# The opening of a two-layer transformer kernel: normalisation in parts, another order of loads and stacks

## The chip, the cores and the metric

The kernel runs on one NeuronCore of a Trainium2 chip. Its time is device microseconds of one execution, and the median of three runs stands for the kernel. In what follows PE is TensorE (PEld its weight load), DVE VectorE, ACT ScalarE, POOL GpSimd and SP SyncE; SPq and ACTq are the queues in which SP and ACT issue DMAs.

## The reference

Two layers act on x of 2048 tokens by 128 channels. Each has an attention and a feed-forward part, each behind a normalisation that is modulated by six vectors from a conditioning vector c:

```python
mod = (silu(c) @ wmod).reshape(1, 6, 1, 128)            # sa, ca, ga, sb, cb, gb
ga = (2 * (ga >= 0) - 1) * maximum(abs(ga), 0.25)       # gb likewise
h = layernorm(x) * (1 + ca) + sa
x = x + ga * attention(h)
h = layernorm(x) * (1 + cb) + sb
x = x + gb * feed_forward(h)
```

Layer 0's attention has 16 heads of 8 channels, is not causal and has biases; its feed-forward part routes each token to one of 16 experts and adds a shared expert. Layer 1's attention is causal, with 8 query heads that share one key and one value head; its feed-forward part mixes each token with the one before. Everything is float32.

## The kernel before, in words

**Opening (L48 to L165).** x goes into SBUF in four blocks of 512 tokens, on SP and ACT in turn (L50 to L52). `load` (L54) brings the small vectors `vec`, the modulation weights `wmod0` and `wmod1` (L65) and 17 weights; 17 of these 20 DMAs are issued on POOL (L59 to L83), and after them POOL makes the identity (`ident`, L89) and the other constants. `last_rows` (L101) is a column with a one in each row 31, 63, 95 and 127. Then (L140 to L164) both layers' modulations are computed: a sigmoid on ACT, six matmuls for each layer (L149, one column each; a float32 matmul stands as two instructions in the records), a copy, two additions and five small steps for each of the two gates on DVE.

**First normalisation.** `layernorm_T` (L168) takes statistics of all 16 tiles of 128 tokens on DVE (L177, L178), one square root on ACT (L179), a reciprocal, and then for each block of four tiles the normalised values (L186), four transposes on PE (L188) and one ACTIVATE with scale and shift into `hT` (L189).

**Layer 0's attention.** `begin0` (L604) makes what the attention reads. Keys are split into a high part and the rest (`split`, L237: hi on ACT, L243; lo on DVE, L244), so that a matmul of rounded operands keeps float32's accuracy. `kS` holds eight *stacks* of 128 rows by 2048 tokens, each for two heads. A stack is first filled with `last_rows` over all its columns (L608, DVE and POOL in turn), and then `stack` (L254) writes four sets of 16 rows into it by DMA (L258): hi, lo, hi, lo of two heads' keys, 128 KB each, 32 in all. hi and lo lie in the memory of `stacks[1]`, which later holds queries. Values are projected by 32 instructions on PE (L631) and a bias added on DVE (L634). `project_q` (L342) does the same as for keys for a block of 512 queries: project (L346), split, and 32 DMAs of 32 KB into `qS`, after a memset on POOL for the first two blocks (L353). hi and lo of a block of queries lie in one buffer each (`qh`, `ql`), so the next block's split waits until these DMAs have read them.

`attention` (L284) works in 16 units, each a block of 512 queries and a group of four heads. Group g reads stacks 2g and 2g+1. The first pass of a unit has 32 steps: two score matmuls on PE (L375, four instructions' worth of 512 columns at most in three PSUM buffers) and a maximum on DVE (L379). Its maxima are then turned (L408) and copied (L409), and SP writes them into the query stack (L412). The second pass computes scores again (L440), takes the exponential on ACT (L450) and weighs the values on PE (L466). `look_ahead` (L557) interleaves them: while unit u makes its second pass, unit u+1 makes its first, and eight steps more (`LEAD`) before unit u's second pass begins. So the first unit's first pass has nothing beside it. A list `late` gives small pieces of other work to every second step; its first entry, in the first unit, is `fold0` (L672), which multiplies the output weights by the gate: two matmuls into a free bank (`fold_gate`, L267, L273), a product on DVE (L275), a copy on ACT (L277), and four additions to x on POOL (L282). `project_q` of the next block is called in the second group's first pass.

**What sets the order.** [...]The framework that builds the program fills these queues by a plan of its own, not in the order of the code: in the trace the product at L271 for layer 1's gate, which the code asks for at the end of layer 0, runs on DVE at 17.07 us between two statistics of the first normalisation.

Of the kernel before, what the change touches and what calls it, by code (L numbers as in the profile page):

```python
# [18 lines left out]
P = 128  # L19
T = 2048  # L20
# [22 lines left out]
def two_layers(ctx: ExitStack, tc: tile.TileContext, a: dict, out: bass.AP):  # L43
# [4 lines left out]
    x = const.tile([P, NT, P], F32, name="x")  # L48
    xv = a["x"].rearrange("(t p) c -> p t c", p=P)
    for b in range(NB):  # L50
        eng = nc.sync if b % 2 == 0 else nc.scalar
        eng.dma_start(out=x[:, b * TB:(b + 1) * TB, :], in_=xv[:, b * TB:(b + 1) * TB, :])  # L52
# [6 lines left out]
    vec = load("vec", [P, NV], nc.gpsimd)  # L59
    modw = ctx.enter_context(ExitStack())  # L60
    wmodp = modw.enter_context(tc.tile_pool(name="wmodp", bufs=1))
    wmod = []
    for layer in range(2):
        t = wmodp.tile([P, 6 * P], F32, name=f"wmod{layer}_sb", tag=f"wmod{layer}")
        nc.gpsimd.dma_start(out=t, in_=a[f"wmod{layer}"])  # L65
        wmod.append(t)
    wk0 = load("wk0", [P, P], nc.sync)
    wv0 = load("wv0", [P, H0 * VW], nc.scalar)
    bv0 = load("bv0", [P, H0 * VW], nc.gpsimd, a["bv0"].partition_broadcast(P))
    wq0 = load("wq0", [P, P], nc.sync)  # L70
    wo0 = load("wo0", [P, P], nc.gpsimd)
    wr0 = load("wr0", [P, NE], nc.gpsimd)
    wsg = load("wsg", [P, NS * P], nc.gpsimd)
    wsu = load("wsu", [P, NS * P], nc.gpsimd)
    wsd = load("wsd", [P, NS, P], nc.gpsimd)
    wk1 = load("wk1", [P, P], nc.gpsimd)
    wv1 = load("wv1", [P, W], nc.gpsimd)
    wq1 = load("wq1", [P, P], nc.gpsimd)
    wq1s = load("wq1s", [P, 4, P], nc.gpsimd)
    wo1 = load("wo1", [P, P], nc.gpsimd)  # L80
    wfr = load("wfr", [P, P], nc.gpsimd)
    wfk = load("wfk", [P, P], nc.gpsimd)
    wfv = load("wfv", [P, P], nc.gpsimd)  # L83
# [5 lines left out]
    ident = const.tile([P, P], F32, name="ident")  # L89
    make_identity(nc, ident)  # L90
    eps = const.tile([P, 1], F32, name="eps")
    nc.gpsimd.memset(eps, 1e-5)
# [6 lines left out]

    last_rows = const.tile([P, 1], F32, name="last_rows")  # L100
    nc.vector.tensor_reduce(last_rows, ident[:, 31::32], AX.X, ALU.add)  # L101
# [35 lines left out]

    mods = []  # L140
    with tc.tile_pool(name="modp", bufs=2, space=PSUM) as mp:
        sg = const.tile([P, 2], F32, name="sg")
        nc.scalar.activation(sg, vcol(V_C0, 2), AF.Sigmoid)
        sc = const.tile([P, 2], F32, name="sc")
        nc.vector.tensor_mul(sc, sg, vcol(V_C0, 2))
        for layer in range(2):
            ps = mp.tile([P, 6], F32, name=f"mod_ps{layer}", tag="mod_ps")
            for j in range(6):
                nc.tensor.matmul(ps[:, j:j + 1], wmod[layer][:, j * P:(j + 1) * P],  # L149
                                 sc[:, layer:layer + 1], start=True, stop=True)  # L150
            m = const.tile([P, 6], F32, name=f"mod{layer}", tag=f"mod{layer}")
            nc.vector.tensor_copy(m, ps)
            for j in (1, 4):
                nc.vector.tensor_scalar_add(m[:, j:j + 1], m[:, j:j + 1], 1.0)
            for j in (2, 5):
                g = m[:, j:j + 1]
                sign = const.tile([P, 1], F32, name=f"sign{layer}{j}", tag=f"sign{layer}{j}")
                nc.vector.tensor_scalar(sign, g, 0.0, 2.0, ALU.is_ge, ALU.mult)
                nc.vector.tensor_scalar_add(sign, sign, -1.0)
# [917 lines left out]
```

## Time and profile before

| | us |
|---|---|
| median of three runs | 1306.71 |
| lowest and highest | 1306.31, 1310.28 |
| the profiled execution | 1276.53 |
| its span, first to last instruction | 1274.8 |

The span is what the profile's views divide; the profiled execution's own time is 1.7 us more. Times in a trace are counted from the start of the span. A group of instructions is given with its number, its busy time and the mean duration of one, where queueing behind others can be part of a duration. The chain of waits follows the work that ended last back from the end; what stands in it set the time.

| from the trace | start us | length us |
|---|---|---|
| first statistics (L177) | 4.39 | 0.26 each |
| identity begun on POOL | 13.46 | 0.22 and 0.32 |
| last block of hT (L189) | 25.91 | 0.78 |
| fills of kS on DVE | 25.91 | 9.71 |
| fills of kS on POOL | 25.95 | 11.43 |
| first key DMA on SP, on ACT | 31.69, 38.08 | |
| first score matmul (L375) | 60.24 | |
| turn of the first unit's maxima (L408) | 101.74 | 1.11 |
| first score of the second pass (L440) | 106.10 | |

### The profile page before, as it was taken

The page shows a single profiled execution, that of the slowest core. Times are in us where ns is not written, and L with a number is a line of the kernel's source. Part 1 is how long each engine was busy: PE and PEld are TensorE (multiplying, and loading weights), DVE is VectorE, ACT ScalarE, POOL GpSimd, SP SyncE. Part 2 cuts the span into 40 slices and gives each one's busy share as a digit, 9 for nine tenths or more (in the row PEclk, how much of TensorE's full clock was granted, in tenths as well). Part 3 has the DMA queues.
Part 4 walks back from the last instruction along what each step waited for, and adds up shares of the span by engine and source line. Part 5 has one row for each costly group of instructions (what it writes and reads, how often), then busy time and mean ns, then how long its engine had stood idle before and what let it go on. Part 6 is the DMA issues. An engine that isn't in the chain of part 4 may idle for free.

```text
span 1274.8 us, 22344 instructions
## 1 busy us (share of the span) xinstructions
PE 1154.6 (91%) x9243; PEld 522.7 (41%) x9243; DVE 967.3 (76%) x1495; ACT 762.8 (60%) x846; POOL 133.6 (10%) x194
## 2 busy tenths in 40 slices
PE   5279999999999999999999999977877999999985
PEld 3223334344333444443344333445643444444432
DVE  5499988899889889888889883173468878898224
ACT  2005777777777777777777778732313455656763
POOL 6401000000000000000000000026251111100113
PEclk9657999999999999999999999987987899999998
DMA  3810000001000001000000000042411001000001
GB/s 115 152 30 18 2 2 2 2 2 35 2 2 1 2 6 32 1 2 2 1 2 2 1 2 2 1 132 54 69 40 34 22 13 35 1 1 1 2 1 33
DMA packets 23700, 27.37 MB, mean 21 GB/s; under 512 B 4960, under 2 KB 17536, under 8 KB 23088
## 3 DMA queue, kind: packets, MB, share of 16 engines
q1 hardware_dynamic: 18512, 16.20, 5.1%
q0 software_dynamic: 2336, 5.48, 2.2%
q10 hardware_dynamic: 2752, 4.27, 1.6%
q8 instruction: 73, 1.20, 0.4%
q14 instruction: 27, 0.22, 0.1%
HBM read 9.88 MB, written 4.13 MB: 11 GB/s over the span
## 4 chain that ended last, share of the span: by engine, by line
PE 76%; DVE 11%; POOL 4%; DMA 3%; issue 3%; ACT 2%; SPq 0%; POOLq 0%; DVEq 0%; ACTq 0%
PE a0bank L466 23%; PE a0p L440 17%; PE a0p L375 12%; PE a1bank L466 5%; PE a1p L440 4%; DVE a0mx L379 3%; PE a1p L375 2%; DVE a1mx L379 2%; PE a1p L446 2%; POOL xs L859 2%; DVE a1masked L384 2%; DMA kS<-a0qS 1%; ACT a0e L450 1%; PE sg L773 1%; POOL kS L608 1%
## 5 line engine op out<-in xcount | busy, mean ns | idle before, releaser
L379 DVE TENSOR_REDUCE a0mx<-a0p 128x2 f32<-128x1024 f32 x512 | 623.7, 1225 | 84.9 <-PE a0p L375 75.6
L450 ACT ACTIVATE a0e<-a0p 128x1024 f32<-128x1024 f32 x512 | 522.3, 1025 | 173.1 <-PE a0p L440 147.2
L466 PE MATMUL a0bank<-a0e,vA 128*32 128x256 f32 x4096 | 333.3, 391 | 0.6 <-ACT a0e L450 0.6
L375 PE MATMUL a0p<-kS,a0qS 64*128 64x512 f32 x1024 | 248.4, 481 | 34.9 <-DMA a0qS<-a0ql 16.8
L440 PE MATMUL a0p<-a0qS,kS 64*128 64x512 f32 x1024 | 259.8, 497 | 0.2 <-DVE a0mx L379 0.2
L450 ACT ACTIVATE a1e<-a1p 128x1024 f32<-128x1024 f32 (+3 forms) x160 | 143.2, 897 | 93.2 <-PE a1p L446 90.3
L440 PEld LDWEIGHTS a0p<-a0qS,kS 64*128 64x128 f32 x1024 | 97.1, 184 | 204.9 <-issue 127.5
L375 PEld LDWEIGHTS a0p<-kS,a0qS 64*128 64x128 f32 x1024 | 100.3, 192 | 120.6 <-ACT a0e L450 58.0
L466 PEld LDWEIGHTS a0bank<-a0e,vA 128*32 128x32 f32 x4096 | 86.3, 108 | 138.6 <-issue 123.8
L379 DVE TENSOR_REDUCE a1mx<-a1p 128x2 f32<-128x1024 f32 x96 | 115.5, 1223 | 18.5 <-PE a1p L375 17.7
L466 PE MATMUL a1bank<-a1e,vA 128*32 128x256 f32 (+1 forms) x1152 | 96.2, 382 | 0.5 <-POOL a1e L453 0.4
L440 PE MATMUL a1p<-a1qS,kS 64*128 64x512 f32 (+3 forms) x320 | 75.1, 463 | 3.6 <-DVE a1mx L379 1.9
L924 POOL MEMSET vA<- 128x16 f32 x1 | 0.1, 127 | 717.9 <-PE a0bank L518 717.9
L375 PE MATMUL a1p<-kS,a1qS 64*128 64x512 f32 (+3 forms) x320 | 67.2, 421 | 6.9 <-DVE a1mx L384 3.9
L384 DVE CUSTOM_DVE_ANT_0 a1masked<-a1p,later 128x128 f32<-128x128 f32 (+3 forms) x128 | 62.6, 489 | 11.9 <-PE a1p L375 7.0
L446 PE MATMUL a1p<-a1mT,a1ones 64*128 64x512 f32 (+3 forms) x320 | 60.6, 371 | 0.0
L440 PEld LDWEIGHTS a1p<-a1qS,kS 64*128 64x128 f32 x320 | 30.7, 187 | 60.6 <-issue 33.4
L453 POOL TENSOR_SCALAR_AFFINE_SELECT a1e<-a1e 128x256 f32<-128x256 f32 x64 | 26.0, 406 | 229.9 <-ACT a1e L450 229.9
L375 PEld LDWEIGHTS a1p<-kS,a1qS 64*128 64x128 f32 x320 | 31.7, 193 | 35.0 <-DVE a1mx L384 9.1
L466 PEld LDWEIGHTS a1bank<-a1e,vA 128*32 128x32 f32 x1152 | 25.2, 108 | 42.1 <-issue 31.7
L446 PEld LDWEIGHTS a1p<-a1mT,a1ones 64*128 64x128 f32 x320 | 31.3, 191 | 1.3 <-issue 1.0
L859 POOL DMA_INDIRECT xs<-hs_rows,tok x31 | 29.6, 955 | 20.3 <-DVE tok L840 11.2
(328 smaller groups left out, 766.1 us busy)
## 6 DMA issues: line engine op xcount, KB each, us to landing
kS<-a0qS SPq DMA_DIRECT2D x16, 128.0 KB
kS<-a0qS ACTq DMA_DIRECT2D x16, 128.0 KB
wgu_sb<-in_gate_up SPq DMA_DIRECT2D x1, 2048.0 KB
a0qS<-a0qh SPq DMA_DIRECT2D x56, 32.0 KB
a0qS<-a0ql SPq DMA_DIRECT2D x56, 32.0 KB
y_rows<-y SPq DMA_DIRECT2D x7, 256.0 KB
a1qS<-a1qh SPq DMA_DIRECT2D x24, 64.0 KB
a1qS<-a1ql SPq DMA_DIRECT2D x24, 64.0 KB
```

Of the source, the lines that this page charges most:

```text
L375: nc.tensor.matmul(ps[:, j, :n], qS[b][r:r + RT, st, i * P:(i + 1) * P], kS(st)[r:r + RT, kb * QB:kb * QB + n], start=True, stop=True)
L379: nc.vector.tensor_reduce(pm[:, i, 2 * pair:2 * pair + 2, kb], ps, AX.X, ALU.max)
L384: nc.vector.tensor_tensor_reduce(masked[:, :n], ps[:, j, :n], later[:, QB - n:], 1.0, LOWEST, ALU.add, ALU.max, pm[:, i, g, kb:kb + 1])
L440: nc.tensor.matmul(ps[:, j, q0:], kS(st)[r:r + RT, kt * P:(kt + 1) * P], qS[b][r:r + RT, st, q0:], start=True, stop=fused)
L446: nc.tensor.matmul(ps[:, j, q0:], ones[r:r + RT, g // S, :], shift[u][r:r + RT, q0:], start=False, stop=True)
L450: nc.scalar.activation(e[:, :, q0:], ps[:, :, q0:], AF.Exp, scale=scale)
L453: nc.gpsimd.affine_select(out=e[:, :, q0:q0 + P], in_=e[:, :, q0:q0 + P], compare_op=ALU.is_ge, fill=0.0, base=0, pattern=[[0, 2], [1, P]] ...
L466: nc.tensor.matmul(av[g * W:(g + 1) * W, c0:c1], vA(kt, grp * HG + g), held[kt, g // 2][:, g % 2, c0:c1], start=(kt == 0 and c0 == 0), sto ...
L608: (nc.vector if st % 2 else nc.gpsimd).tensor_copy(kS[:, st, :], last_rows.to_broadcast([P, T]))
L773: nc.tensor.matmul(ps[:, j, :], w[:, k * P:(k + 1) * P], hT[:, b * QB:(b + 1) * QB], start=True, stop=True)
L859: nc.gpsimd.indirect_dma_start(out=xs[:, j, :], out_offset=None, in_=a["hs_rows"], in_offset=bass.IndirectOffsetOnAxis(ap=tok[:, j:j + 1], ...
L924: nc.gpsimd.memset(vA1[:, :, D1:D1 + 1], 1.0)
```

## The change

- Loads: none on POOL. SP and ACT issue them in order of need: x's first block, `vec`, the second block, `wmod0`, the third and fourth, then the key and query weights on ACT and all others on SP. `wmod0` and `wmod1` are kept for the whole kernel. `ident`, `eps` and `last_rows` come first on their engines.
- Fills: `kS0` is allocated ahead of the normalisation. All eight fills are ACTIVATEs on ACT (`fill`), two of them before the normalisation, six between the stacks.
- First normalisation: `first_norm` replaces `layernorm_T` here. For each of the four blocks `start` takes statistics and a square root, `end` the reciprocal, values, transposes and the ACTIVATE; block b+1 is started ahead of b's end. PSUM holds two blocks.
- Modulation: layer 0's (`modulation(0)`) stands after the first `start`; its gates come at the end of `begin0`. Layer 1's, with its gates, is computed in `fold0`, in the bank that `fold_gate` uses.
- Stacks: the first block's queries are projected and stacked in `begin0`, next to the keys. Stacks 0 and 1 use SP and ACT, the other six SP alone, in order of stack: four key DMAs, then four query DMAs. The memset for the first block's query stack stands at the beginning of `begin0`.

The core of the diff:

```diff
-    for b in range(NB):
-        eng = nc.sync if b % 2 == 0 else nc.scalar
-        eng.dma_start(out=x[:, b * TB:(b + 1) * TB, :], in_=xv[:, b * TB:(b + 1) * TB, :])
...
-        nc.gpsimd.dma_start(out=t, in_=a[f"wmod{layer}"])
...
+    load_x(0, nc.sync)
+    vec = load("vec", [P, NV], nc.scalar)
+    load_x(1, nc.scalar)
+    wmod = [load("wmod0", [P, 6 * P], nc.sync)]
+    load_x(2, nc.sync)
+    load_x(3, nc.scalar)
+    wk0 = load("wk0", [P, P], nc.scalar)
+    wq0 = load("wq0", [P, P], nc.scalar)
+    wv0 = load("wv0", [P, H0 * VW], nc.sync)
+    bv0 = load("bv0", [P, H0 * VW], nc.sync, a["bv0"].partition_broadcast(P))
+    wmod.append(load("wmod1", [P, 6 * P], nc.sync))
...
+    def modulation(layer, ps):
+        if layer == 0:
+            nc.scalar.activation(sg, vcol(V_C0, 2), AF.Sigmoid)
+            nc.vector.tensor_mul(sc, sg, vcol(V_C0, 2))
+        for j in range(6):
+            nc.tensor.matmul(ps[:, j:j + 1], wmod[layer][:, j * P:(j + 1) * P],
+                             sc[:, layer:layer + 1], start=True, stop=True)
+        m = const.tile([P, 6], F32, name=f"mod{layer}", tag=f"mod{layer}")
+        nc.vector.tensor_copy(m, ps[:, :6])
+        for j in (1, 4):
+            nc.vector.tensor_scalar_add(m[:, j:j + 1], m[:, j:j + 1], 1.0)
+        mods.append(m)
...
-            kS, vA, q0 = begin(ep, ps_s, stacks)
+            qS = {}
+            kS, vA, qS[0] = begin(ep, ps_s, stacks)
...
-                          (nc.sync, nc.scalar) if b == 0 else (nc.sync,), step)
+                          (nc.sync,), step)
...
-    layernorm_T(h, HOFF, m[:, 1:2], m[:, 0:1], "ln0")
...
+    def first_norm():
+
+        with tc.tile_pool(name="ln0", bufs=2) as wp, \
+                tc.tile_pool(name="ln0p", bufs=2, space=PSUM) as pp:
+            got = {}
+
+            def start(b):
...
+                for i in range(TB):
+                    nc.vector.bn_stats(stats[:, i, :], x[:, b * TB + i, :])
+                    nc.vector.bn_aggr(mv[:, i, :], stats[:, i, :])
+                rstd = wp.tile([P, TB], F32, name=f"ln0rstd{b}", tag="rstd")
+                nc.scalar.activation(rstd, mv[:, :, 1], AF.Sqrt, bias=eps)
+                got[b] = mv, rstd
+
+            def end(b):
+                mv, rstd = got.pop(b)
+                nc.vector.reciprocal(rstd, rstd)
+                xn = normal(b, f"ln0{b}", mv, rstd)
+                turn_normal(pp.tile([P, QB], F32, name=f"ln0ps{b}", tag="ps"), xn,
+                            hT[:, b * QB:(b + 1) * QB], mods[0][:, 1:2], mods[0][:, 0:1])
+
+            start(0)
+            modulation(0, pp.tile([P, 6], F32, name="mod_ps", tag="mod_ps"))
+            for b in range(NB):
+                if b + 1 < NB:
+                    start(b + 1)
+                end(b)
...
+    kS0 = pool.tile([P, H0 * RT // P, T], F32R, name="kS0", tag="kS")
+
+    def fill(st):
+
+        nc.scalar.activation(kS0[:, st, :], last_rows.to_broadcast([P, T]), AF.Copy)
+
+    for st in range(2):
+        fill(st)
+    first_norm()
...
-        for st in range(nst):
-            (nc.vector if st % 2 else nc.gpsimd).tensor_copy(kS[:, st, :],
-                                                             last_rows.to_broadcast([P, T]))
+        kS = kS0
+        nc.gpsimd.memset(stacks[0].bitcast(F32), 0.0)
...
+        ps = pp.tile([P, 2, QB], F32, name="pq0", tag="s")
+        nc.tensor.matmul(ps[:, 0, :], wq0, hT[:, :QB], start=True, stop=True)
+        split(ps[:, 0, :], vcol(V_BQ), qhi, qlo)
...
-            stack(kS[:, st, :], (hi[rows], lo[rows]), (0, 1, 0, 1), (nc.sync, nc.scalar), RT // D0)
+            queues = (nc.sync, nc.scalar) if st < 2 else (nc.sync,)
+            if st >= 2:
+                fill(st)
+            stack(kS[:, st, :], (hi[rows], lo[rows]), (0, 1, 0, 1), queues, RT // D0)
+            stack(stacks[0][:, st, :], (qhi[rows], qlo[rows]), (0, 0, 1, 1), queues, RT // D0)
...
+        gates(0)
...
     def fold0(bank):
+        modulation(1, bank)
+        gates(1)
         wog, rows = fold_gate(pool, bank, wo0, vcol(V_BO), m[:, 2:3], "a0")
```

## The prediction

> **What bounds the kernel now.** I read the page first, then busy time by stretches of time, then the chain of waits from 24 to 62 us, then the queues of SP and ACT. The page: TensorE is the bound of the whole.
>
> ```profile
> span 1274.8 us, 22344 instructions
> PE 1154.6 (91%) x9243; PEld 522.7 (41%) x9243; DVE 967.3 (76%) x1495; ACT 762.8 (60%) x846; POOL 133.6 (10%) x194
> PEclk9657999999999999999999999987987899999998
> ```
>
> An average hides stages. Stretches of layer 0 (columns: stretch, length, busy us with number of instructions for PE, PEld, DVE, ACT, POOL, granted clock, DMA share, GB/s):
>
> ```profile
> 26.00:38.00 12.00, 6.06 (x18) 3.04 (x16) 12.00 (x7) 3.50 (x4) 12.00 (x6) 0.90 0.41 63
> 38.00:56.00 18.00, 5.44 (x25) 5.17 (x24) 4.12 (x11) 0.00 (x0) 4.10 (x3) 0.59 0.96 182
> 61.00:103.00 42.00, 30.09 (x81) 11.34 (x80) 41.93 (x40) 0.80 (x2) 0.91 (x1) 0.50 0.13 29
> 120.00:290.00 170.00, 168.72 (x1494) 67.84 (x1492) 151.91 (x141) 128.29 (x130) 0.00 (x0) 1.00 0.01 2
> ```
>
> From 120 us on PE is busy 168.7 of 170 us: a unit of attention takes about 44.8 us there, and nothing of this change takes TensorE work out of it. Before that, in turn: DVE and POOL full (26 to 38), DMA full with PE nearly empty (38 to 56), DVE full at half clock (61 to 103, the first unit's first pass, whose maxima nobody has computed ahead). So the opening 60 us is a chain of its own, and what it loses shifts everything behind it. The chain of waits there:
>
> ```profile
> 25.95 11.43 POOL kS L608 x4
> 38.08 4.38 DMA kS<-a0qS
> 42.53 4.44 DMA kS<-a0qS
> 47.05 5.14 DMA kS<-a0qS
> 52.27 3.20 DMA kS<-a0qS
> 58.35 1.90 DMA a0qS<-a0ql
> 60.25 0.80 PE a0p L375 x2
> ```
>
> POOL fills kS for 11.4 us, then 32 key transfers of 128 KB come in rounds of eight, about 4.4 us each, then the query stacks. The first unit reads only two of the eight stacks. The fills (mean of one in ns) and the modulation:
>
> ```profile
> L608 POOL CAST kS<-last_rows 128x2048 fp32r<-128x2048 f32 x4 | 11.4, 2892 | 3.6 <-PE ln0ps L188 3.6
> L608 DVE CAST kS<-last_rows 128x2048 fp32r<-128x2048 f32 x4 | 9.7, 2488 | 1.9 <-PE ln0ps L188 1.9
> L149 PE MATMUL mod_ps<-sc,wmod_sb 128*128 128x1 f32 x24 | 5.3, 352 | 8.3 <-DMA wmod_sb<-in_wmod 8.3
> ```
>
> They wait for the last transpose of the normalisation (ln0ps): fills come after it, not beside it. Later on SP's queue:
>
> ```profile
> 70.12 9.97 SPq L258 DMA_DIRECT2D a0qS<-a0qh  x16
> 103.49 1.21 SPq L412 DMA_DIRECT2D a0qS<-a0mT  x2
> ```
>
> One queue alone issues a DMA in 0.62 us (9.97/16); L412, which the first unit's second pass waits for, comes 43.2 us after the first L375.
>
> [...]The trace agrees on the load (1.28 us at L143, L179 and L450); 128x1024 with a bias took 1.11 us at L243. [...]side by side three of DVE's four fills took about 2.9 us, the shortest 1.23. [...]The trace: 0.62 us alone on SP, two queues at 0.6 each.
>
> **The change, part by part.**
> *Loads by need.* POOL's 17 issues (1.32 to 13.5 us) go to SP and ACT. What it frees is ident, at 13.46 before, now about 2 us; last_rows with it. SP's 19 loads at 0.5 us each are 9.5 us in an idle queue (2.8 to 31.7 us before); ACT's five at 0.53 keep it until 3.5 us. The first x landed at 4.4 us with all in flight, wmod0 at 8.2; now about 4 and 6 to 7. No gain of its own unless the normalisation follows.
>
> *Normalisation in parts.* The 16 statistics (0.26 + 0.08 us) stood behind the modulation's copy on DVE and ended at 17.3. Now one table load (1.28), fills 0 and 1 on ACT (2 x 1.89) and up to two more loads run 3.5 to about 11; Sigmoid there, then 12 passes of modulation (a float32 matmul is two in the records) at 0.22 us (5.27/24) to about 14, copy and additions 0.4. Four blocks of transposes (0.28 each) and Identity (0.78) through two PSUM buffers, one about 1.0 us after the other: hT complete at 18.5, 20.5 if one fill of a later stack comes between; before, 26.7. Moving gates (0.07 us apart on DVE, ten) off this path saves under 1 us, inside that figure; the later gates lie in DVE's wait for stacks.
>
> *Fills and split.* The last key projection (four passes, 0.5 to 0.93 us each at full or half clock: two were 1.86 us at 23.8, 1.02 at 25.7), hi on ACT 1.11, lo on DVE 1.27: lo is ready at 22 to 24.3. Before, lo stood behind 9.7 us of DVE's fills and ended at 38.0. POOL's and DVE's fills (11.4 us on the path) are gone; six of ACT's eight, 11.3 us, lie in its idle time (before: nothing on ACT from 31.6 to 69.4 but DMA issues); uncovered each costs 1.9 us.
>
> *First group first.* 8 key and 8 query DMAs instead of 32 and the query's. Two rounds: four of 128 KB and four of 32 KB each. A round of 1 MB took 4.4 us, one small DMA 1.9 to landing; so about 3.2 to 3.5 us a round: stack 0 at 26 to 28, stack 1 at 29 to 31.5. The value projections (32 passes at 0.206 us = 6.6, 6.58 for 28 before) fill PE meanwhile until about 28. The second step needs stack 1, so the pass counts as begun 1.13 us before it: **29.5 us**, instead of 60.2. That is 30.7 us less.
>
> *The other six stacks.* 24 key and 24 query DMAs, all on SP: 48 x 0.62 = 29.8 us, from 27 to 57. They lie beside the first pass (33 reductions took 37.4 us), which reads the next stacks only after 32 steps, at about 66. Behind them on SP stand the 16 hi DMAs of the next queries (10 us, they also wait for POOL's 3.5 us memset, as in before) and then L412: 27 + 64 x 0.62 = 67, plus some 3 us of waits for memset and qh; due at 29.5 + 43.2 = 72.7. Cost nothing, with 3 us of cover.
>
> *Layer 1's modulation.* 12 passes x 0.22 = 2.6 us on PE, in bank 0 after the turn of unit 0, next to the fold (L273), copy and about 12 small DVE steps. Part may hide while L412's transfer is under way (103.5 to 106.1), part may add a wait of up to 1.2 us for a reduction in front of the copy; behind it on PE wait L440 and L375. Not shown by this trace, so: 0 to 4.5, I take 2.6. The fold's rows go to POOL, which waited 47 us.
>
> Sum: 30.7 - 2.6 = **28 us**. On the profiled execution (1276.5, its span and 1.7 around it) 1248.5. The median of the runs is 1306.7, 30.2 above it; I cannot see why, and the change acts on a stretch with no dense TensorE work, so I carry the difference over as microseconds: **1279**.
>
> **Rivals.** *ACT becomes the wait (1287).* Queues here are ordered by the framework's own plan: a product for layer 1's gate (L271) ran at 17.07 between statistics. It may put later fills ahead of Sigmoid, Identity or hi. Three on the path and two table loads: 3 x 1.9 + 2 x 1.28 = 8.3 us. For it: [...]eight fills are ready from 2 us. Against: gaps of waiting take some.
> *SP becomes the wait (1285, at the worst rate seen 1295).* With 0.8 us a DMA, L412 comes at 27 + 51 + 0 to 3 = 78 to 81, 5.5 to 8.5 late. SP's 16 key DMAs took 15.44 us in before, 0.965 each, with ACT's beside them: at that rate 16 us late.
> *No change (1308).* The first L375 waits for all stacks after all: about 59 us, and the modulation is added. Against: in before L375 began at 60.2, while query stacks were still issued until 69.
> *Slower (1316).* The same SP queue, beyond its point: L412 late by more than 28 us eats the gain, that is over 1.15 us a DMA; at 1.3, 27 + 83 - 72.7 = 37 late, 9 slower. [...]landings of 4.4 us with eight under way speak against it.
>
> **Numbers.** Forecast 0.60 (own range 1274 to 1284: start 26 to 31.5, modulation 0 to 4.5); ACT 0.14; SP 0.18; no change 0.03; slower 0.05. From these: faster by over 0.3% (3.9 us, about what a measurement of this kernel can tell from no change) 0.92, within 0.03, slower 0.05. The range 1273 to 1291 takes in forecast, ACT, and SP up to 0.9 us a DMA.
>
> **What would show it.** First L375 at 26 to 29 us, reductions without gaps from the second on; no L608 on DVE or POOL, eight fills of about 1.9 us on ACT; hT complete by 20; L412 some 43 us after the first L375, not waiting in SP; 12 passes next to L273. Wrong if reductions of the first pass pause for DMA, if L412 follows mT by more than 1 us, or if unit times after 120 us change.

## The result

| | median us (runs) | lowest to highest |
|---|---|---|
| before | 1307.19 (7) | 1303.08 to 1311.66 |
| after | 1296.39 (7) | 1289.81 to 1299.44 |

The ratio is 0.9912, with a 95% interval of 0.9888 to 0.9936: faster by 11.5 us (8.4 to 14.6). A second series gave 0.9886 (0.9856 to 0.9916). The direction was right, but the time lies 17 us above the forecast and 5 above the top of the range.

The profiled execution of after took 1296.39 us, span 1294.7. The profile of before that the prediction was read from (span 1274.8) was an unusually short execution; a second profile of the same kernel has a span of 1310.5, close to the median. Of the 35.7 us between those two 30.6 lie in the routed experts, where the change does nothing (shown under the second run of before), so the opening is compared in both.

The head of the page of after, as it answers to that of before:

```profile
span 1294.7 us, 22355 instructions
PE 1166.7 (90%) x9243; PEld 528.8 (41%) x9243; DVE 958.2 (74%) x1494; ACT 776.4 (60%) x857; POOL 112.3 (9%) x173
PEclk9659999999999999999999999876976799999998
```

TensorE is still the bound of the whole; DVE and POOL lost the fills, ACT gained them. The stretches, with the columns of the prediction (the third stretch is moved to where the first pass lies now):

```profile
26.00:38.00 12.00, 6.79 (x37) 4.78 (x35) 6.47 (x11) 3.63 (x3) 0.00 (x0) 1.00 0.69 109
38.00:56.00 18.00, 10.75 (x30) 4.28 (x30) 14.47 (x13) 3.71 (x2) 0.00 (x0) 0.53 0.83 106
43.00:85.00 42.00, 30.22 (x81) 11.53 (x77) 41.70 (x40) 0.57 (x1) 0.00 (x0) 0.50 0.69 79
120.00:290.00 170.00, 168.72 (x1482) 68.66 (x1478) 151.32 (x149) 126.96 (x131) 0.00 (x0) 1.00 0.02 6
```

From 26 to 38 us DVE is no longer full (6.47 us for 12.00) and POOL does nothing. The first pass fills DVE from 43 to 85 us, 41.70 of 42, where before it did so from 61 to 103. From 120 to 290 us TensorE is busy as long as before, to the hundredth (168.72 us). What stands in the opening now is told by the chain of waits, from 12 us to the first score matmul after which the reductions have no more gaps (start, length, work; "..." stands for lines left out):

```profile
12.72 1.91 ACT kS L638
...
18.53 1.80 ACT kS L638
...
23.51 1.12 PE pq L656 x2
24.64 3.43 PE pk L664 x8
...
29.05 2.38 DVE a0qS L246 x2
...
32.01 6.07 DMA kS<-a0qS
...
38.63 3.17 DMA kS<-a0qS
...
41.92 0.81 PE a0p L377 x2
```

Fills on ACT (at 12.72, 14.81, 18.53 and 20.99; two are shown) stand between the blocks of the normalisation, all projections that the first unit reads follow the last block of `hT`, and then come 9 us of transfers, where before had 22 (38.08 to 60.25). At the other end of the first unit, TensorE (idle time and its releaser in brackets):

```profile
84.48 2.72 PE L108 MATMUL a0bank<-sc,wmod_sb 128*128 128x1 f32 x12
...
89.31 0.79 PE L275 MATMUL a0bank<-ident,mod 128*128 128x128 f32 x2 [1.39 <-DVE mod L111]
...
90.46 0.79 PE L442 MATMUL a0p<-a0qS,kS 64*128 64x512 f32 x2
```

Layer 1's modulation is there, 2.72 us, and its copy made TensorE wait another 1.39. The first score of the second pass moved from 106.10 to 90.46: 15.6 us.

Three marks split the opening, and every run below is read by them. **hT** is the end of its last ACTIVATE; **lo** the end of the last key split; **start** the begin of the first pass on DVE, counted back from the first of its reductions that follow one another without a gap, 1.23 us (the duration of one) for each earlier one. **L442** is the first score of the second pass, and **unit** the distance from start to it.

| us from the span's start | hT | lo | start | L442 | unit |
|---|---|---|---|---|---|
| before, first profile | 26.7 | 38.0 | 61.1 | 106.1 | 45.0 |
| before, second profile | 27.0 | 38.3 | 61.7 | 106.7 | 45.0 |
| forecast for after | 18.5 to 20.5 | 22 to 24.3 | 30.3 | | +2.6 |
| after | 23.5 | 31.4 | 41.5 | 90.5 | 48.9 |
| after, second profile | 24.0 | 32.0 | 42.3 | 91.3 | 48.9 |

The forecast's 29.5 is the begin of the first L375; in before the first reduction stood 0.8 us behind that (60.24 and 61.07), so on the scale of this table it is 30.3. The start came 11.2 us later, in three parts: hT 4.0 late (against the middle, 19.5), from hT to lo 4.3 more than forecast (8.0 for 3.7), from lo to start 2.9 more (10.1 for 7.2). The unit grew by 3.9 us, 1.3 more than forecast.

### The profile page after: what moved, and what is told of

Its sections match the earlier page's. It is cut to its first block, busy times and chain, and to the rows that moved or that the text cites. A ratio compares the mean times of both kernels' runs of the same rounds, so it can differ in the third digit from the quotient of the medians.

```text
span 1294.7 us, 22355 instructions
## 1 busy us (share of the span) xinstructions
PE 1166.7 (90%) x9243; PEld 528.8 (41%) x9243; DVE 958.2 (74%) x1494; ACT 776.4 (60%) x857; POOL 112.3 (9%) x173
## 4 chain that ended last, share of the span: by engine, by line
PE 77%; DVE 11%; ACT 4%; issue 3%; another core or an unknown queue 2%; DMA 1%; POOL 1%; POOLq 0%; ACTq 0%; DVEq 0%; SPq 0%
PE a0bank L468 23%; PE a0p L442 17%; PE a0p L377 12%; PE a1bank L468 5%; PE a1p L442 4%; DVE a0mx L381 3%; PE a1p L377 2%; DVE a1mx L381 2%; PE a1p L448 2%; DVE a1masked L386 2%; PE sg L826 2%; ACT a0e L452 1%; PE gu L935 1%; PE a0bank L499 1%
## 5 line engine op out<-in xcount | busy, mean ns | idle before, releaser
L442 PE MATMUL a0p<-a0qS,kS 64*128 64x512 f32 x1024 | 259.8, 497 | 0.0
L442 PEld LDWEIGHTS a0p<-a0qS,kS 64*128 64x128 f32 x1024 | 97.1, 184 | 204.3 <-issue 128.8
L381 DVE TENSOR_REDUCE a1mx<-a1p 128x2 f32<-128x1024 f32 x96 | 115.6, 1222 | 20.8 <-PE a1p L377 19.9
L442 PE MATMUL a1p<-a1qS,kS 64*128 64x512 f32 (+3 forms) x320 | 76.4, 472 | 3.1 <-DVE a1mx L381 1.9
L442 PEld LDWEIGHTS a1p<-a1qS,kS 64*128 64x128 f32 x320 | 31.1, 190 | 60.9 <-issue 33.4
L935 PE MATMUL gu<-wgu_sb,xsT 128*128 x62 | 18.5, 451 | 20.0 <-issue 19.5
L411 ACT CAST a0mT<-a0bank 8x512 fp32r<-8x512 f32 x16 | 9.2, 574 | 45.4 <-PE a0bank L410 45.3
```

The costliest lines, as they stand in the source:

```text
L381: nc.vector.tensor_reduce(pm[:, i, 2 * pair:2 * pair + 2, kb], ps, AX.X, ALU.max)
L411: nc.scalar.copy(mT, ps[:nm_rows])
L442: nc.tensor.matmul(ps[:, j, q0:], kS(st)[r:r + RT, kt * P:(kt + 1) * P], qS[b][r:r + RT, st, q0:], start=True, stop=fused)
L935: nc.tensor.matmul(ps[:, i, :], xsT[q][:, i * P:(i + 1) * P], wgu[:, bass.ds(regs[j], 1), :].rearrange("p a f -> p (a f)"), start=True, st ...
```

## The experiments

My theory after the result: fills on ACT delay the normalisation, the projections wait for all of it, and the key transfers of the first group are slower than I took them. The rivals: the ACT queue doesn't matter and the transfers set the start alone; or the whole gain is the order of the stacks, and the normalisation in parts brings nothing. All times are ratios to before on the same chip (95% interval); the runs are from four chips, and where the intervals of two versions overlap, the marks tell them apart, not the ratios.

### The pair again: again_before, after_again

No edit.

> The kernel before, unchanged, profiled a second time. Theory (the profile of before that the prediction was built on was of an unusually short execution): the profile now ends near 1305 us; attention 0 ends at 827 us as before, and the missing 28 us appear between there and the first score pass of attention 1 (959 us in the old profile, about 987 now), as an idle PE in the routed experts. Rival (the pause in the routed experts belongs to the change): the profile ends near 1275 us again and first score pass of attention 1 is at 959 us.

> The kernel after, unchanged, measured a second time. Theory (the opening's 15 us are the whole gain, and the first ratio, 0.9912, lay at one end of its spread): ratio 0.987 to 0.9895 to the kernel before, 14 to 17 us; in the profile the first pass runs without gaps from 41 to 42.5 us and the first second-pass score is at 90 to 91. Rival (some 4 us of the opening's gain are lost again behind the first unit): ratio 0.9905 to 0.993 again.

Before, again: 0.999 (0.9965 to 1.0014), median 1309.77. After, again: 0.9886 (0.9856 to 0.9916), 1293.78 beside 1309.57. Of the 30.6 us that the second profile of before takes longer in the experts, 26.0 lie in front of one row, TensorE's product of the routed experts, here from the groups of before's first and second profile and of after (busy us, mean ns; then idle time ahead of it, and what ended it):

```profile
L882 PE MATMUL gu<-wgu_sb,xsT 128*128 x62 | 16.7, 417 | 1.1 <-issue 0.5 <-DVE acte L753 0.2 <-ACT xsT L870 0.2
```

```profile
L882 PE MATMUL gu<-wgu_sb,xsT 128*128 x62 | 18.4, 448 | 27.1 <-ACT xsT L870 26.0 <-DVE acte L753 0.5 <-issue 0.5
```

```profile
L935 PE MATMUL gu<-wgu_sb,xsT 128*128 x62 | 18.5, 451 | 20.0 <-issue 19.5 <-DVE acte L806 0.5
```

One wait of 26.0 us in the second profile, of 19.5 in after, none in the first. All other profiles have it, at 17 to 26 us, but for early_proj's, which ran on another chip (there before takes 1284.51 us). In the chain of waits it stands between two neighbouring ACTIVATEs of ACT and is put down to an unknown queue. It belongs to both kernels, so nothing of the change explains it; what it waits for stays open. From the last weighting of attention 0 to the first pass of attention 1 it is 163.6 us in before's second profile and 161.3 in after: what the opening gained (16.3 us at L442 and 15.2 at the end of attention 0, 827.3 to 812.1) was not lost again.

### The order of stacks alone, and the rest alone: stacks_only, norm_only

stacks_only is before with after's `begin0` (stack order, fills on ACT, queries stacked beside keys); loads, normalisation and modulation are before's. norm_only is after, with the stacks in the old order:

```diff
+        for st in range(2, nst):
+            fill(st)
...
-            queues = (nc.sync, nc.scalar) if st < 2 else (nc.sync,)
-            if st >= 2:
-                fill(st)
-            stack(kS[:, st, :], (hi[rows], lo[rows]), (0, 1, 0, 1), queues, RT // D0)
-            stack(stacks[0][:, st, :], (qhi[rows], qlo[rows]), (0, 0, 1, 1), queues, RT // D0)
+            stack(kS[:, st, :], (hi[rows], lo[rows]), (0, 1, 0, 1), (nc.sync, nc.scalar), RT // D0)
+        for st in range(nst):
+            rows = slice(st * 2 * D0, (st + 1) * 2 * D0)
+            stack(stacks[0][:, st, :], (qhi[rows], qlo[rows]), (0, 0, 1, 1),
+                  (nc.sync, nc.scalar), RT // D0)
```

> The kernel before, with one part of the change alone: the first group's stacks first, the others on SP's queue during the first unit, fills on ACT; loads, first normalisation and both modulations as before. Theory (this part carries nearly the whole gain: 24 of the 32 key DMAs, 0.7 us each, leave the opening, and DVE is rid of its fills ahead of lo): last lo at 33 to 35 us instead of 38, start of the first pass at 43 to 46 instead of 60.5, 15 to 17 us earlier, time 1291 to 1294 us. Rival (normalisation in parts is what counts, as its forecast share of 18 us of 31 said): lo stays at 38, start at 48 to 50, 1297 to 1299 us.

> The kernel after without its stack order: all key stacks first, then all query stacks, on both queues as before; loads by need, normalisation in parts, fills on ACT and layer 1's modulation in the first unit stay. Theory (the parts of the opening other than the stack order bring some 6.5 us of start, of which the moved modulation takes 3.8): last lo at 31.4, start at 52.5 to 54.5 us instead of 60.5, time 1305 to 1307 us where the kernel before has 1309. Rival (they bring their forecast 14 to 16 us): start at 45 to 47, 1296 to 1299 us.

| | hT | lo | start | L442 | unit | ratio |
|---|---|---|---|---|---|---|
| stacks_only | 26.6 | 34.3 | 44.1 | 89.3 | 45.1 | 0.9886 (0.9861 to 0.991) |
| norm_only | 23.9 | 33.4 | 60.3 | 106.4 | 46.1 | 1.0026 (1.0007 to 1.0044) |

The order of the stacks, with the fills on ACT that stacks_only has too, is worth as much as the whole change: 17.0 and 17.6 us of start against before's two profiles. Everything else by itself gains nothing: in norm_only hT and lo come 3 and 5 us earlier, and the start only 0.8 and 1.4. As norm_only has the same fills, it is the order that makes the difference, 18.8 us of start from norm_only to after; the order with the old fills was not run. The chain of norm_only says why:

```profile
34.20 6.10 DMA kS<-a0qS
...
40.32 6.34 DMA kS<-a0qS
...
46.72 5.26 DMA kS<-a0qS
...
52.00 4.97 DMA a0qS<-a0ql
...
59.45 0.80 PE a0p L377 x2
```

From 34.20 us to the first score matmul the links are transfers and the issuing of them, nothing else. The DMA queues between 31 and 57 us, before first and then norm_only (packets, MB, share of 16 engines):

```profile
DMA packets 1042, 4.23 MB, mean 163 GB/s; under 512 B 513, under 2 KB 513, under 8 KB 530
q10 hardware_dynamic: 497, 2.10, 45.5%
q1 hardware_dynamic: 545, 2.13, 45.0%
```

```profile
DMA packets 1096, 4.28 MB, mean 165 GB/s; under 512 B 542, under 2 KB 542, under 8 KB 584
```

Both move 4.2 to 4.3 MB at 163 to 165 GB/s, in before with 90.5% of the DMA engines' time taken (45.5 + 45.0). And both begin within 0.5 us of each other: the first key DMA needs hi and the fill of its stack, not lo, and was issued on SP at 31.69 in before, at 31.2 in norm_only. There the second hi ended at 31.18 in spite of the earlier hT, since a fill on ACT (26.66 to 28.56) and slow projections (2.08 us for the two passes at 23.96, where after's took 1.12) stood in front of it. So the 3 us of hT were lost ahead of the transfers already, and the 5 us of lo bought nothing because the transfers were not waiting for lo: SP's had begun under the old fills, beside which they ran from 31.7 to 37.4 us. The moved modulation costs norm_only as much as after, but not where the mark of the unit looks: its copy ran at 108.89, behind the first L442 (106.38), so the unit shows 46.1, and attention 0 ended 3.7 and 2.5 us later than in before's two profiles in spite of the earlier start.

In after the two parts overlap: with the stacks in order, the new normalisation brings the start from 44.1 to 41.5, 2.6 us, and the modulation that moved with it costs 3.8 in the unit (48.9 for 45.1).

### Layer 1's modulation back in front: mod1_early

```diff
             modulation(0, pp.tile([P, 6], F32, name="mod_ps", tag="mod_ps"))
+            modulation(1, pp.tile([P, 6], F32, name="mod_ps1", tag="mod_ps"))
...
         gates(0)
+        gates(1)
...
     def fold0(bank):
-        modulation(1, bank)
-        gates(1)
```

> The kernel after, with layer 1's modulation and gates back in the opening. Theory (twelve passes and a copy cost 3.8 us between the first pass and the second in the first unit, and in the opening they lie in PE's waits): start of the first pass unchanged within 1 us at 41 to 42.5, first second-pass score 45 us after it instead of 48.8, time 1292 to 1293.5 us. Rival (the cost in the unit is a wait that something else ends): the distance stays 48 to 49 us and the time 1296. Second rival (the twelve passes and their load push the opening): start 2 us or more later, 1295 to 1297.

Start 42.0, unit 45.1, L442 at 87.1; ratio 0.9877 (0.9847 to 0.9907).

The 3.8 us of the unit are gone, and the start is 0.4 us later, less than the 0.6 to 0.8 us by which two profiles of one kernel differ here. So the modulation belongs where it was: in after's opening TensorE waits anyway (it is busy for 8.82 of the first 23.50 us).

### Fills elsewhere: fills_pool, hold_fills, fills_late, best_late

fills_pool writes the fills as before, but all on POOL. hold_fills ties fills 2 to 7 to the last key split, so that ACT can't take them early; fills_late ties fills 0 and 1 to the last block of hT as well; best_late is fills_late with mod1_early.

```diff
# fills_pool
-        nc.scalar.activation(kS0[:, st, :], last_rows.to_broadcast([P, T]), AF.Copy)
+        nc.gpsimd.tensor_copy(kS0[:, st, :], last_rows.to_broadcast([P, T]))
# hold_fills
-    def fill(st):
+    def fill(st, rows=last_rows):
...
+            if st == 2:
+                late_rows = pool.tile([P, 1], F32, name="late_rows", tag="late_rows")
+                nc.vector.scalar_tensor_tensor(late_rows, lo[:, T - 1:T].bitcast(F32), 0.0,
+                                               last_rows, ALU.mult, ALU.add)
...
-                fill(st)
+                fill(st, late_rows)
# fills_late, besides
-    for st in range(2):
-        fill(st)
...
+        hT_rows = pool.tile([P, 1], F32, name="hT_rows", tag="hT_rows")
+        nc.vector.scalar_tensor_tensor(hT_rows, hT[:, T - 1:T], 0.0, last_rows,
+                                       ALU.mult, ALU.add)
+        for st in range(2):
+            fill(st, hT_rows)
```

> The kernel after, with all eight key fills on POOL instead of ACT, otherwise unchanged. Theory (the fills stand in ACT's queue in front of the third square root, the activations that write hT and the splits): hT is complete at 18.5 to 20 us instead of 23.5, the last lo at 26 to 27.5 instead of 31.4, the first pass runs without gaps from about 37 instead of 41.6, 4 to 5 us earlier, and the time is 1291 to 1293 us where the kernel after has 1296.4. Rival (the fills only use ACT's idle time; transposes, projections and the DMAs set the start): hT is complete at 23 and the first pass starts at 41 to 42 as in the kernel after, 1296 us. Third (POOL's fill of 2.9 us is too slow for stack 1): start at 43 or later, above 1298.

> The kernel after, but the fills of stacks 2 to 7 read a column that is made from the last lo, so that they and the DMAs of these stacks come after the splits. Theory (the fills delay the splits on ACT, and stack 2's DMAs go out among the first group's): the last lo at 27 to 28.5 us instead of 31.4, the DMA phase from lo to the gapless first pass 6 to 7.5 us instead of 10.2, start at 34 to 36 instead of 41.6, time 1289 to 1291 us. If only the fills matter: lo at 28, the DMA phase still 10, start 38, 1293 us. Rival (the later stacks are now late for the first pass): its reductions pause for stacks 2 to 7 by more than 3 us in sum and the time is 1296 us or more.

> The kernel after, with no fill on ACT ahead of the last hT: fills 0 and 1 read a column made from the last hT, fills 2 to 7 one made from the last lo. Theory (two fills at 12.7 us delay the third square root by some 3 us and with it half of hT): hT complete at 19.5 to 20.5 us instead of 23.5, the last lo at 27.5 to 29.5 instead of 31.4, gapless first pass from 36 to 38.5 instead of 41.6, time 1290 to 1293 us. Rival (TensorE is still at half clock that early, so the projections take what the normalisation saves): hT at 20, but pq and pk take 7 us instead of 4.6 and lo is done at 30 or later; start 38.5 to 40, time 1293 to 1295 us. Second rival (the DMAs set the start whatever lo does): start at 41 or later.

> As fills_late, and layer 1's modulation and gates back in the opening. Theory (both losses add up): start of the first pass as in fills_late within 1.5 us, first second-pass score 45 us after it, time 4 us below fills_late and 7 to 10 us below the kernel after: 1286 to 1289 us. Rival (the twelve passes push the opening's chain now that the fills no longer cover them): start 2 to 3 us later than in fills_late, time as in the kernel after with layer 1's modulation back, 1291 to 1292.

| | hT | lo | start | L442 | unit | ratio |
|---|---|---|---|---|---|---|
| fills_pool | 34.7 | 43.4 | 53.4 | 102.3 | 48.9 | 0.9984 (0.9969 to 0.9999) |
| hold_fills | 23.0 | 32.4 | 39.9 | 88.9 | 48.9 | 0.9869 (0.9838 to 0.99) |
| fills_late | 20.6 | 28.6 | 37.8 | 86.8 | 48.9 | 0.9874 (0.9845 to 0.9904) |
| best_late | 21.7 | 31.3 | 39.7 | 84.8 | 45.1 | 0.986 (0.9836 to 0.9883) |

fills_late moved hT from 23.5 to 20.6, close to the late end of the forecast (20.5), and the start to 37.8: the fills on ACT cost the normalisation about 3 us. hold_fills alone moved hT by only 0.5 us, since fills 0 and 1 stayed in front, and its lo came at 32.4 for an expected 27 to 28.5; its start gained 1.6 us later, in the transfers. best_late's L442 is 5.7 us ahead of after's, but its lo came 2.7 us later than in fills_late. Here the expected rival came half true: 1.0 us of it is hT, which the twelve passes in front of the transposes delay now that no fill covers them. The rest is TensorE's clock: best_late's first two projections took 2.07 us and the next eight 4.41, where fills_late's took 1.12 and 3.60. The eight of hold_fills and of fills_late:

```profile
24.89 5.08 PE L664 MATMUL pk<-hT,wk_sb 128*128 128x512 f32 x8
```

```profile
21.61 3.60 PE L662 MATMUL pk<-hT,wk_sb 128*128 128x512 f32 x8
```

The same eight passes, with no wait between them, took 5.08 us and 3.60. In the trace the first record of a full clock is at 27.9 us in hold_fills and at 20.0 in fills_late; in after at 22.2, in best_late at 25.2, in before at 25.5 and 27.3. Ahead of its first record a trace shows no clock; in after two passes took 1.91 us there (at 19.23) and 1.12 behind it (at 23.51), so I call it half (in warm_proj, at a recorded half clock, two took 2.08).

fills_pool fell for a reason that neither theory had. POOL's fills take 1.89 us, as ACT's do in after (1.90), but look at the normalisation's values on DVE, first in after, then in fills_pool, and at what POOL does then:

```profile
13.20 1.08 DVE L222 TENSOR_SCALAR ln01xn<-x,ln0mv,ln0rstd 128x128 f32<-128x128 f32 x4
```

```profile
13.27 7.48 DVE L222 TENSOR_SCALAR ln01xn<-x,ln0mv,ln0rstd 128x128 f32<-128x128 f32 x4
```

```profile
12.83 1.89 POOL L638 CAST kS<-last_rows 128x2048 fp32r<-128x2048 f32 x1 [8.17 <-DVE last_rows L96]
```

Four TENSOR_SCALARs take 7.48 us instead of 1.08, and the next four 6.97, while POOL goes from fill to fill (1.89 each, with a memset of 3.51 between them). The first of the four ended at 14.79, the fill at 14.72. Block 0's four, at 11.40, ahead of all fills, took 1.10; those of the last block, at 31.69, when POOL's fills had just ended, 1.58. So a TENSOR_SCALAR beside POOL's work took about seven times as long here; by what means POOL holds DVE up is not shown. In after the four ran beside a fill on ACT (12.72 to 14.63) and took 1.08: ACT was the right engine for the fills; only their place was wrong.

### Which queue carries which stack: after_cross, best_cross, stacks_cross

```diff
-            queues = (nc.sync, nc.scalar) if st < 2 else (nc.sync,)
+            queues = (nc.scalar,) if st == 1 else (nc.sync,)
```

The same edit on after, on best_late and on stacks_only: SP moves stack 0, ACT stack 1, where each had half of both.

> The kernel after with one edit: all of stack 0's DMAs on SP's queue and all of stack 1's on ACT's, where both queues shared each stack. Theory (the four key DMAs of one stack read the same 16 partitions and pass one after the other, 1.25 us to a packet of 8 KB; of two stacks at once a packet takes 0.65 us, as where both queues were busy in the kernel before): the phase from the last lo to the gapless first pass shrinks from 10.2 us to 5.5 to 8, start at 37 to 39.5 us instead of 41.6, time 1291 to 1294 us. Rival (the 16 DMA engines are full whatever the order; the phase is the number of key DMAs times 0.83 us): start at 41 to 42 as in the kernel after, 1296 us. Second rival (stack 1 now waits for ACT, whose queue has fills ahead): start later than 42, above 1297.

> best_late with the same edit of the queues. Theory (as in after_cross, and nothing else is in these DMAs' way): phase from the last lo to the gapless first pass 5 to 6.5 us instead of 8.3, start at 36 to 38 us instead of 39.7, time 1287 to 1289 us. Rival (the DMA engines are full): start at 39 to 40, 1291 us.

> stacks_only (the kernel before with the stack order alone) with the same edit of the queues. Theory: start at 40 to 42 us instead of 44.1, time 1289 to 1292 us where stacks_only has 1293, so that the stack order with its queues gains more than the whole change. Rival (the DMA engines are full): start at 44, 1293 us.

| | lo | start | lo to start | without the edit | ratio |
|---|---|---|---|---|---|
| after_cross | 31.9 | 40.5 | 8.6 | 10.1 | 0.9868 (0.9849 to 0.9887) |
| best_cross | 29.5 | 37.1 | 7.6 | 8.3 | 0.9832 (0.9807 to 0.9857) |
| stacks_cross | 35.6 | 43.3 | 7.7 | 9.8 | 0.9857 (0.9833 to 0.9881) |

The phase is shorter by 0.7 to 2.1 us in all three, less than expected in the first two (8.6 for 5.5 to 8, 7.6 for 5 to 6.5), and stacks_cross started at 43.3 for an expected 40 to 42. The ratios alone do not show the edit: those of best_cross and stacks_cross overlap with best_late's and stacks_only's, after_cross's with after's second. best_cross, at 1287.88 us, has the lowest ratio so far: its interval (up to 0.9857) lies below after's first one (from 0.9888) and just touches the second (from 0.9856). The reason shows in what the DMA engines take for a byte. One queue alone, in after:

```profile
DMA packets 882, 2.49 MB, mean 96 GB/s; under 512 B 434, under 2 KB 434, under 8 KB 626
q1 hardware_dynamic: 882, 2.49, 86.1%
```

That is 50 to 76 us: 86.1% of 16 engines for 26 us is 358 us of engine time for 2.49 MB, 144 us a MB. In before, from 31 to 57 us, two queues with different stacks took 90.5%, 376 us for 4.23 MB, 89 us a MB. In the engines' own records the median packet of 8 KB takes 1.26 us in the first case and 0.65 in the second. The four key DMAs of one stack all read the same 16 partitions. The phase from lo to start, in stacks_only (34.3 to 44.1 us) and in stacks_cross (35.6 to 43.3), shows the same with two queues:

```profile
DMA packets 415, 1.17 MB, mean 119 GB/s; under 512 B 210, under 2 KB 210, under 8 KB 293
```

```profile
DMA packets 448, 1.18 MB, mean 154 GB/s; under 512 B 225, under 2 KB 225, under 8 KB 330
```

The same bytes move at 119 GB/s when both queues share a stack and at 154 when each has its own, so the rival, DMA engines that are full whatever the order, falls. So a second queue brought more at another stack than at the same one; whether the 16 partitions that one stack's DMAs share are the cause is not shown by itself. The prediction looked at a second queue for its issue time alone (0.62 us a DMA on SP, 0.6 each with two queues); here it brought more.

### Projections inside the normalisation, and a warm clock: early_proj, warm_proj

early_proj is best_cross with the normalisation called from `begin0`, in the projections' own PSUM buffers, so that each projection can follow its block of hT; warm_proj adds three matmuls at the start of TensorE's queue, whose result nobody reads.

```diff
-    first_norm()
+        def project(b):
+            if b == 0:
+                ...
+            if b % 2:
+                ...
+        first_norm(pp, project)
...
+            for i in range(3):
+                nc.tensor.matmul(ps[:, i % 2, :], later[:, :P], later, start=True, stop=True)
```

> best_cross, and the first normalisation takes its PSUM tiles from the pool of the projections, so that the first query projection and the first two key projections no longer wait until the last transposed block has been read out of a pool that lies in the same banks. Theory (that wait put all projections behind the last hT, where the forecast had only the last one there): the first key split before the last hT, the last lo at 26 to 27.5 us instead of 29.5, gapless first pass from 33.5 to 35.5 us instead of 37.1, time 1284 to 1287 us. Rival (the key DMAs of the first two stacks set the start, not lo): lo at 26 to 27.5 but start at 36.5 to 37.5, 1288 us. Second rival (the projections at half clock now delay the later transposes): lo at 29 or later, 1288 us or more.

> early_proj with three multiplications of a constant tile, whose result nobody reads, on TensorE from 2.4 us on, where it had nothing to do until 7.6 us. Theory (the half clock of TensorE until about 20 us sets the opening once ACT is free): the granted clock is full from 7 to 13 us on, the query projection takes 1.0 us instead of 2.07 and four key passes 1.8 instead of 3.1, hT complete at 21 to 22.5 us instead of 24.9, the last lo at 26 to 27.5 instead of 29.9, gapless first pass from 34 to 36 instead of 38, 2 to 4 us below early_proj's ratio of 0.9819: 0.979 to 0.981. Rival (the key DMAs hold the start however early lo is): lo at 26 to 27.5, start at 37 to 38.5. Second rival (the clock falls back in the waits between the passes, or the extra passes push the modulation): lo at 29.5 or later, ratio 0.982 or more.

| | hT | lo | start | L442 | ratio |
|---|---|---|---|---|---|
| best_cross | 21.5 | 29.5 | 37.1 | 82.2 | 0.9832 (0.9807 to 0.9857) |
| early_proj (another chip) | 24.9 | 29.9 | 38.1 | 83.2 | 0.9819 (0.9792 to 0.9846) |
| warm_proj | 27.0 | 31.9 | 39.2 | 84.3 | 0.9829 (0.98 to 0.9857) |

The wait of the projections was real, and it went: the queries' projection ran at 15.56 us, where best_cross had 21.52, and lo followed hT by 4.9 us, not 8.0. But lo came no earlier, because hT was later: six passes in front of the remaining transposes took 2.07 and 3.11 us, for the most part ahead of the first record of a full clock at 20.8. From TensorE's timeline, warm_proj's first projection:

```profile
17.48 2.08 PE L666 MATMUL pq<-hT,wq_sb 128*128 128x512 f32 x2 [0.87 <-ACT hT L230]
```

2.08 us for two passes that took 1.12 in after; early_proj's took 2.07. warm_proj was to lift the clock. Its six passes ran from 2.44 to 7.2 us, the clock was full at 6.3, 3.9 us after the first of them, but half again at 9.7, long before the first projection, and full only at 23.4:

```profile
6.30:9.70 3.40, 2.38 (x14) 1.46 (x13) 3.17 (x20) 1.77 (x3) 1.79 (x1) 1.00 0.99 257
9.70:20.00 10.30, 6.54 (x22) 4.67 (x23) 6.36 (x54) 2.15 (x6) 1.81 (x4) 0.50 0.47 140
```

In the 3.40 us at full clock TensorE worked for 2.38, its longest wait was 0.85, and the clock fell all the same. What brought it down stays open. In this opening, full of waits, the work done ahead did not keep the clock. warm_proj lost more besides: layer 1's modulation, which stands in front of block 0's last transpose, began at 13.58, 3.0 us later than in early_proj. Clock and modulation are the second of the expected rivals. Whether a full clock through the opening would help stays open; no run had one.

## Why the prediction was half right

**Right.** The order of the stacks was the lever: stacks_only gained 17.0 to 17.6 us of start with it. SP's cover was right in kind: L414 was issued at 84.04, right behind the copy of the turned maxima (83.44 to 84.01), and no reduction of the first pass paused for a transfer, so the SP rival and the slower one fell. SP did take longer for a stack DMA than the 0.62 us of the forecast: the last 43 ran from 39.80 to 76.84, 0.86 us each. That cost nothing because the 16 DMAs of the next queries, which the forecast had put ahead of L412, came behind it, from 99.67 on. The 1.89 us for a fill on ACT were my estimate, which no trace of before shows; measured, a fill took 1.90. Carrying the 30.2 us between profile and median over as microseconds held, since most of them lie in the experts; when it was done no cause was known, so that was luck. The time from unit to unit did not change behind the first (on average 45.2 us in both).

**Step "Normalisation in parts" (hT at 18.5 to 20.5): 4.0 us late.** I let one fill stand among the blocks at the outside. `last_rows` came from DVE only at 12.56 us, behind statistics, so fills 0 and 1 started at 12.72, not at 3.5, and the first four fills ran ahead of and between the Identities, with the third Sqrt (17.19) behind two of them. That is the ACT rival, at half its price, with the late `last_rows` as its cause; fills_late took 2.9 us of the 4.0 away. That work behind a waiting instruction waits with it, on which this rival rests, shows here on ACT: it did nothing for the 4.63 us before fill 0, and a cast (L159), whose input POOL had written by 3.63, ran only behind that fill, at 14.53.

**Step "Fills and split" (lo at 22 to 24.3): 4.3 us more.** I let only the last key projection follow hT. All of them do, 1.12 + 3.43 us after 23.51, because the normalisation's PSUM buffers lie where the projections' will, and those wait until all of it is released; the projection of the next block's queries (L348), in another bank, ran at 19.2. early_proj moved them forward, so the wait is shown; it changed the buffers and the place of the calls together, so that the buffers are its cause is supported by L348, not shown by itself. About 1 us of the 4.3 is the fill on ACT at 25.72, which stood in front of the first hi: the passes that hi reads ended at 26.35, and it began at 27.52. early_proj gained nothing, as its first six passes took 5.18 us, 0.86 each, where after's two took 1.12. I had both rates of a pass in the prediction and did not carry the slow one on.

**Step "First group first" (lo to the first L375 in 6.3, to the first reduction in 7.2): 2.9 us more.** I priced two rounds by a round of before, 1 MB in 4.4 us; but that is the time one DMA took to land, and the line for 38 to 56 us has 182 GB/s, 5.8 us for 1 MB. And SP's plan put the four key DMAs of stack 2 among those of the first group, eight from 29.66 to 39.76 us, and a round in which both queues take one stack was slower than one over two stacks (119 GB/s in stacks_only, 154 in stacks_cross). Crossing the queues gave 1.5 of it back, hold_fills (fills 2 to 7 later, and with them stack 2's DMAs on SP) 2.6 (from 10.1 to 7.5, though its lo came 1.0 us later).

**Step "Layer 1's modulation" (2.6, bounds 0 to 4.5): 3.9.** The passes were as priced (2.72 for 2.6); the term that I had left in the bounds and put at nothing in the sum, a wait for the copy behind a reduction, was 1.39.

**The sum** is then 28 less 11.2 less 1.3: 15.5 us, and L442 moved by 15.6 and 16.3 against before's two profiles. The two timed series gave 11.5 and 14.9, with intervals of 8.4 to 14.6 and 11.0 to 18.9. The forecast's own range was added up wrongly: starts of 26 to 31.5 and a modulation of 0 to 4.5 give 1272.5 to 1282.5, not 1274 to 1284; the measured 1296.4 lies outside both.

**The attribution** was wrong where the sum hides it. The forecast read the chain of before as fills and then transfers, let the transfers start 15 us earlier with the normalisation and fills, and counted that as gain; but SP's transfers had begun at 31.69, beside the fills. In norm_only nothing of the 15 us arrives: hi, which lets the first key DMA go, comes 0.4 us earlier than in before, and 32 key DMAs follow as before. With the stacks in order 2.6 us arrive, less than the modulation that was moved with it costs. Stacks alone are as fast as after (0.9886); with the fills late, the modulation early and the queues crossed, it is 0.9832.

## What to carry to other kernels

When several things stand in front of one start, change each alone before adding up their lengths: here the order of the transfers was worth about 17 us of start and a normalisation 3 us earlier 1 to 2.6, because the transfers had long begun when the last of their inputs was ready. A fill on an "idle" engine can stand on the path if its input arrives in the midst of a chain that uses the engine, so tie it to an input that comes when the chain is over. Price a matmul in an opening at the clock that its own stretch shows (two passes of the projection took 1.12 us in after, 2.08 in warm_proj), and a group of DMAs at the rate measured for its kind (119 GB/s here with both queues at one stack, 154 with a stack for each).

## What was not expected of the hardware

- Beside POOL's copies of 128x2048 (1.89 us each) and a memset (3.51) four DVE TENSOR_SCALARs took 7.48 us in fills_pool; in after, without them, 1.08.
- A packet of 8 KB took 1.26 us (median) when one queue's DMAs read the same 16 partitions (after, 50 to 76 us), 0.65 when two queues worked at different stacks (before, 31 to 57).
- TensorE had no full clock on record until 22.2 us in after and 25.5 in before, though it had work in pieces, and it had half the clock from 39.3 to 100.7 in after and from 45.9 to 114.2 in before, through the whole first pass, in which it was busy for 30.22 of 42 us in after. The stretches at one clock between changes last multiples of 3.41 us in both, such as 17.07 and 61.44 in after. The first change came at other times in runs of nearly the same kernel (20.0 us in fills_late, 27.9 in hold_fills), and with it a projection of eight passes took between 3.60 and 5.08 us. Only warm_proj had the full clock before 20 us, for 3.41 us.
- Of the 16 profiles 14 have a pause of 17 to 26 us in the experts; before's first and early_proj's have none. Its cause is open.
